# One gather in eighteen replaced by column copies on ScalarE and VectorE in a graph message-passing kernel

## The chip, the cores and the metric

The kernel runs on one core of one Trainium2 chip. The time is the device time of one execution in microseconds. The profile is of one execution on the same chip, with the same five engines that the text names throughout: PE (matmuls, with PEld for its weight loads), DVE (VectorE), ACT (ScalarE), POOL (GpSimd) and SP (which here only issues DMAs). Each engine takes its own instructions in order and waits for the others on semaphores.

## The reference

One layer of a graph network on 12,500 nodes with 64 features and 200,000 edges with 32 features, all float32. The edges are sorted by destination.

```python
msg_in = jnp.concatenate([nodes[row], nodes[col], edge_features], axis=-1)
messages = _mlp(msg_in, mW1, mb1, mW2, mb2)
aggregated = jax.ops.segment_sum(messages, col, num_segments=nodes.shape[0])
upd_in = jnp.concatenate([nodes, aggregated], axis=-1)
return _mlp(upd_in, uW1, ub1, uW2, ub2)
...
x = _layernorm(x + _L0_gnn_ref(x, src, dst, edge_attr_32, ...), axis=-1)
```

`_mlp(x, W1, b1, W2, b2)` is `relu(x @ W1 + b1) @ W2 + b2` with 128 hidden units. `row` is the source of an edge (random over all nodes), `col` its destination.

## The kernel before

The first message layer is split by its three inputs. A table A holds `x @ W1a` for every node (128 numbers each, in HBM), a table B holds `x @ W1b + b1`, and the edge features are multiplied by their part of W1 as they come. An edge's hidden vector is then relu(A[source] + B[destination] + edge part).

**Tiles.** 128 edges are one tile; 1,563 tiles. Six tiles (SUB) are one step, 261 steps; the text calls a step by its number s. Two steps (SUP, twelve tiles) share one selection and one load of edge features; they are number g, and j is 0 or 1 for the first or second step of the two.

**A step**, in the order in which the main loop (the `for s in range(last + 3)` loop) issues it:

- `gather` (L168), on POOL: one indirect DMA per tile takes 128 rows of A by the tile's source numbers. The first ten steps (XG) gather rows of x itself instead. 18 row buffers (ROWB) let POOL run ahead of the rest.
- `windows(s + 2)`, on SP: because destinations are sorted, a tile's destinations lie in a window of 32 rows of B. SP loads six window numbers into registers (L224) and issues six small DMAs into `rhs` (L229), each with a register operation that makes its address.
- `node_part(s)`: DVE adds the gathered rows to the matmul result, h = pc + xg (L276), ACT applies the relu (L277).
- `collect(s - 1)`, on PE: h times a selection matrix adds the tile's hidden vectors into a running sum by destination (L302), and a second matmul counts edges (L307). Six offsets come from registers that PE loads (L298).
- Every second step `select` makes a 0/1 matrix that tells the destination within the window (`l`, L196) and another for the sums (`sel`, L200), `load` brings edge features into the other rows of `l` (L215), and ACT makes a bfloat16 copy of `sel` (`counts`, L208). `loadd` (L184) brings the destination numbers that `select` compares.
- `edge_part(s + 1)`, on PE: one matmul per tile, `l` against `rhs` (L256), which gives B's row and the edge part together in `pc`. `pc` has two buffers.
- Updates: the running sums are closed 33 times, in steps that lie further apart at the start (47 steps) than at the end (4). An update takes two matmuls with 448 columns (`update`, L337 and L338), a relu, eight matmuls (`residual`, L346 and L347), DVE's statistics (L351, L353), a square root on ACT (L355), and the normalization (L364).

The order is written by hand (`manual_schedule`): each engine gets its instructions in the program's order, and only the semaphores are derived. During steps 11 to 50 PE also makes table B piece by piece (`chunk_b`).

Of the kernel before, what the change touches and what calls it, by code (L numbers as in the profile page):

```python
# [10 lines left out]
F32 = mybir.dt.float32  # L11
# [6 lines left out]
P = 128  # L18
# [6 lines left out]
SUB = 6  # L25
# [15 lines left out]
EARLY = NCH * P  # L41
GE = 26
BS = 11
UB = 4
NCOL = (-(-N // P) + UB) * P
UN = 448
# [17 lines left out]


@with_exitstack
def gnn_kernel(ctx: ExitStack, tc: tile.TileContext, x1T, x, eT, e_rows, src, dst, dst_row, wrow, wnext, whalf,
               mW1, mb1, mW2, mb2, uW1, ub1, uW2, ub2, out):

# [31 lines left out]
    K = len(UPD)  # L101

    src_s = const.tile([P, NT], I32, name="src_s")
    wint = const.tile([1, NTP], I32, name="wint")
    past = const.tile([1, 1], F32, name="past")

    xall = const.tile([P, -(-NB // NCH), HB * P], F32, name="xall")
# [30 lines left out]
    flag_i = const.tile([1, 1], I32, name="flag_i")  # L138
    usup = const.tile([1, K], I32, name="usup")
    ustep = const.tile([1, K], I32, name="ustep")  # L140
    woff = const.tile([1, NTP], I32, name="woff")
    wh = const.tile([P, NTP // 2], I32, name="wh")
    wa = const.tile([SUP, NSUP], I32, name="wa")
    wb = const.tile([SUP, NSUP], I32, name="wb")
# [9 lines left out]
    def tiles(s):  # L154
        return range(s * SUB, min((s + 1) * SUB, NT))

    def gather(s):

        if s >= XG or s % 2 == 0:
            buf = rows.tile([P, SUB, DH], F32, name="xg")  # L160
        else:
            buf = xg[s - 1][0]
        if s < XG:
            a = buf.rearrange("p k (b d) -> p (k b) d", d=D)[:, s % 2 * SUB:(s % 2 + 1) * SUB, :]
        else:
            a = buf.rearrange("p (b k) d -> p k b d", b=2)
        for i, t in enumerate(tiles(s)):
            nc.gpsimd.indirect_dma_start(  # L168
                out=a[:, i, :] if s < XG else a[:, i // 2, i % 2, :], out_offset=None, in_=A[:, :] if s >= XG else x[:, :],
                in_offset=bass.IndirectOffsetOnAxis(ap=src_s[:, t:t + 1], axis=0))  # L170
        xg[s] = buf, a

    with tc.tile_pool(name="sup", bufs=2) as sup, tc.tile_pool(name="work", bufs=2) as work, tc.manual_schedule():
        L, S, SB, xs, hs, pcs, sums = {}, {}, {}, {}, {}, {}, {}
        pt = psum.tile([P, SUB // 2, P], F32, name="pt", tag="sums")

# [63 lines left out]
        def parts(n):  # L240

            if n == SUB:
                return [(slice(0, 2), SUB // 2)]
            return [(slice(b, b + 1), (n - b + 1) // 2) for b in range(2) if n > b]

        def edge_part(s):

            n = len(tiles(s))
            g, j = divmod(s, SUP // SUB)

            pc = psum.tile([P, 2, 4, DH], F32, name="pc")[:, :, :SUB // 2]
            for i in range(n):
                k, b = divmod(i, 2)
                q, m = 64 * b, j * SUB // 2 + k

                nc.tensor.matmul(pc[:, b, k, :], L[g][q:q + 64, m, :], rhs[g % 2][q:q + 64, m, :],  # L256
                                 start=s >= XG or k == 0, stop=s >= XG)
            pcs[s] = pc

        def node_part(s):  # L260

            n = len(tiles(s))
            pc = pcs.pop(s)
            h = work.tile([P, 2, SUB // 2, DH], F32, name="h")
            if s < XG:
                xt = xs.pop(s)
                for i in range(n):
                    k, b = divmod(i, 2)
                    q = 64 * b
                    nc.tensor.matmul(pc[:, b, k, :], xt[q:q + 64, k, :], w1a[q:q + 64], start=False,  # L270
                                     stop=i + 2 >= n)
                nc.scalar.activation(h, pc, AF.Relu)
            else:
                a = xg.pop(s)[0].rearrange("p (b k) f -> p b k f", b=2)
                for b, m in parts(n):
                    nc.vector.tensor_tensor(h[:, b, :m], pc[:, b, :m], a[:, b, :m], op=ALU.add)  # L276
                    nc.scalar.activation(h[:, b, :m], h[:, b, :m], AF.Relu)  # L277
            hs[s] = h

        def opened(u):  # L280
# [37 lines left out]
        def close(u):  # L318

            ps, pn = sums.pop(u)  # L320
            nc.scalar.copy(sums_s[u % 2], ps)
            nc.scalar.copy(xw[u % 2][0:1, :UW], pn)

        us = {}

# [158 lines left out]
        for k, c in enumerate(range(0, NB, NCH)):  # L484
            chunk_a(c)
            if k == 0:
                chunk_b(0, [B0v, Bv])
            if k == 2:

                w0 = wint[:, :GE * SUP]  # L490
                nc.vector.tensor_scalar(past, w0[:, GE * SUP - 1:], float(EARLY - WIN), None, op0=ALU.is_gt)
                nc.vector.tensor_scalar(w0, w0, float(EARLY - WIN), None, op0=ALU.min)
                windows(0)
                windows(1)
            if k == 4:
                relative(0, 8 * SUP)
            if k == 6:
                offsets()
            if k == 9:
                select(0)  # L500
                load(0)
                counts(0)

        def rest(s):

            if s == 1:
                relative(8 * SUP, 8 * SUP + WCH)
            elif s == 2:
                relative(8 * SUP + WCH, NT)
                halves(4 * SUP, NTP // 2)  # L510
            elif s == BS:
                nc.sync.dma_start(wa, wrow.rearrange("o (p c) -> (o p) c", c=NSUP))
                nc.sync.dma_start(wb, wnext.rearrange("o (p c) -> (o p) c", c=NSUP))
                nc.scalar.dma_start(w2, mW2)
                nc.scalar.dma_start(u1a, uW1[D:2 * D, :])
                nc.scalar.dma_start(b2c, mb2.rearrange("(f o) -> f o", o=1))
                nc.vector.memset(uz[:D], 0.0)
                nc.vector.memset(ux[:D], 0.0)
                nc.vector.memset(eps, EPS)
                nc.vector.memset(ones, 1.0)  # L520
                nc.vector.tensor_copy(ux[D:], ident[D:, D:])
# [61 lines left out]
        for s in range(last + 3):  # L583
            g, j = divmod(s, SUP // SUB)
            while gathered < NSUB and frees(gathered) < s:
                gather(gathered)
                gathered += 1
            if s - 2 in due:
                norm(due[s - 2])
            if s + 2 < NSUB:  # L590
                windows(s + 2)
            if s < NSUB:
                node_part(s)
            if 1 <= s <= NSUB:
                collect(s - 1)
            if s + 1 in due:
                close(due[s + 1])
            if j == 0 and g + 1 < NSUP:
                select(g + 1)
                load(g + 1)  # L600
                counts(g + 1)
            if j == 1 and g + 2 < NSUP:
                loadd(g + 2)
            if chunks and s >= BS and chunks[0] < NCH + NB * (s + 1 - BS) / (SUP // SUB * (GE - 1) - BS):
                chunk_b(chunks.pop(0), [Bv])
            if s + 1 < NSUB:
                if s + 1 < XG:
                    transpose(s + 1)
                edge_part(s + 1)
            if s in due and due[s] + 1 < K:  # L610
                carry(due[s] + 1)
            if s in due:
                update(due[s])
            if s - 1 in due:
                residual(due[s - 1])
            if s + 2 in due:
                columns(due[s + 2])
            rest(s)
            if s - 2 in due:
                store(due[s - 2])  # L620
# [166 lines left out]
```

## Time and profile before

| | us |
|---|---|
| median of three runs | 1979.92 (1979.69 to 1980.9) |
| the profiled execution | 1980.06 |
| its span | 1978.3 |
| PE busy | 1520.7 (77%) |
| DVE busy | 554.1 (28%) |
| ACT busy | 359.1 (18%) |
| POOL busy | 1476.7 (75%) |
| granted TensorE clock, mean | 0.53 |
| DMA, mean | 105 GB/s |

Busy is the time in which the engine's datapath works on an instruction. Register operations, register loads and semaphore waits, which an engine's sequencer does itself, are not in it. The profile's groups give a line, an engine, an operation, the output and inputs, how often it ran, then busy time and mean duration in ns, and after the bar the idle time just before those instructions and what ended most of it.

### The profile page before, as it was taken

How to read it: one execution, taken by the hardware profiler on the slowest of the kernel's cores; microseconds unless marked ns; L12 is line 12 of the kernel's file. 1: busy time of each engine (PE TensorE's matmuls, PEld its weight loads, DVE VectorE, ACT ScalarE, POOL GpSimd, SP SyncE). 2: the span in 40 equal slices, each digit the busy share in tenths (PEclk: the TensorE clock that was granted, in tenths of full speed). 3: DMA queues.
4: the chain of work that ended last, by engine and by line, in shares of the span. 5: the costliest groups of instructions: out<-in, count | busy, mean ns of one | idle time of the engine just before them, and what ended most of it. 6: DMA issues, size and time to landing. Idle time of an engine off the chain costs nothing.

```text
span 1978.3 us, 34854 instructions
## 1 busy us (share of the span) xinstructions
PE 1520.7 (77%) x9218; PEld 1321.6 (67%) x9218; DVE 554.1 (28%) x1165; ACT 359.1 (18%) x550; POOL 1476.7 (75%) x1572
## 2 busy tenths in 40 slices
PE   3796898876757676776777777778778888888987
PEld 2696787765656665666666666667666777777766
DVE  1423333322222322222222232222222323323322
ACT  0221111211111111111111111111112112122121
POOL 7777777777777777777777777777777777777774
PEclk8655555555555555555555555555555555555555
DMA  8634454433333333333333333333333333333332
GB/s 207 181 97 120 130 134 126 115 103 92 98 94 95 94 98 98 94 96 99 96 98 96 101 92 100 101 97 99 100 99 98 99 103 97 101 102 100 101 103 63
DMA packets 244063, 208.45 MB, mean 105 GB/s; under 512 B 78233, under 2 KB 208370, under 8 KB 243875
## 3 DMA queue, kind: packets, MB, share of 16 engines
q0 software_dynamic: 50016, 100.57, 20.3%
q1 hardware_dynamic: 179312, 96.69, 17.8%
q10 hardware_dynamic: 14546, 8.93, 1.6%
q8 instruction: 88, 1.44, 0.3%
q14 instruction: 101, 0.82, 0.1%
HBM read 188.25 MB, written 17.69 MB: 104 GB/s over the span
## 4 chain that ended last, share of the span: by engine, by line
POOL 53%; issue 28%; PE 9%; DMA 7%; DVE 1%; SPq 1%; ACT 0%; ACTq 0%; DVEq 0%; POOLq 0%
POOL xg L168 53%; PE sums L302 4%; DMA xg<-tab_a,src_s 4%; PE pc L256 3%; DMA tab_a<-tb 1%; PE pb L410 1%; DMA l<-in_eT 1%; DMA w1b<-in_mW 1%; SPq L229 1%; PE pc L270 1%; PE pt L236 0%; PE cnt L307 0%; DMA rhs<-tab_b 0%; DMA xall<-in_x1T 0%; DVE tb L418 0%
## 5 line engine op out<-in xcount | busy, mean ns | idle before, releaser
L168 POOL DMA_INDIRECT xg<-tab_a,src_s x1503 | 1418.5, 944 | 460.5 <-issue 449.8
L302 PEld LDWEIGHTS sums<-sel,h 128*128 128x128 f32 x3126 | 669.6, 320 | 365.3 <-ACT h L277 316.4
L302 PE MATMUL sums<-sel,h 128*128 128x32 f32 x3126 | 689.5, 391 | 278.7 <-ACT h L277 265.9
L276 DVE TENSOR_TENSOR h<-pc,xg 128x768 f32<-128x768 f32 x252 | 239.5, 951 | 1043.7 <-DMA xg<-tab_a,src_s 812.8
L256 PE MATMUL pc<-rhs,l 64*128 64x128 f32 x3126 | 444.2, 439 | 95.4 <-DVE h L276 54.2
L256 PEld LDWEIGHTS pc<-rhs,l 64*128 64x128 f32 x3126 | 366.6, 318 | 120.2 <-DVE h L276 58.0
L277 ACT ACTIVATE h<-h 128x768 f32<-128x768 f32 x252 | 211.2, 839 | 1116.6 <-DVE h L276 1055.0
L196 DVE TENSOR_TENSOR l<-l,cps 128x768 f32<-128x768 int32 (+1 forms) x134 | 127.8, 954 | 98.5 <-DMA l<-in_dst_row 94.8
L208 ACT CAST selb<-sel 128x384 bf16<-128x384 f32 x131 | 66.7, 509 | 181.0 <-DVE sel L200 167.7
L346 PE MATMUL py<-ux,xw 128*128 128x64 f32 x264 | 84.5, 423 | 1.6 <-DVE h L276 1.6
L307 PE MATMUL cnt<-selb,one 128*1 128x32 bf16 x1563 | 85.3, 189 | 0.0
L347 PE MATMUL py<-u,hTu 128*128 128x64 f32 x264 | 82.9, 417 | 0.4 <-ACT hTu L339 0.4
L337 PE MATMUL pu<-sums_s,w2u 128*128 128x448 f32 x66 | 61.4, 1034 | 22.3 <-DVE h L276 21.6
L200 DVE TENSOR_TENSOR sel<-cps,drc 128x384 f32<-128x384 f32 x131 | 71.8, 548 | 20.0 <-PE sums L302 19.9
L346 PEld LDWEIGHTS py<-ux,xw 128*128 128x128 f32 x264 | 69.9, 324 | 9.5 <-issue 7.6
L347 PEld LDWEIGHTS py<-u,hTu 128*128 128x128 f32 x264 | 71.2, 329 | 0.6 <-ACT hTu L339 0.6
L168 POOL DMA_INDIRECT xg<-in_x,src_s x60 | 57.1, 952 | 19.1 <-issue 18.0
L307 PEld LDWEIGHTS <-one 128*1 128x1 bf16 x1563 | 54.3, 83 | 23.0 <-issue 8.7
L351 DVE BATCH_NORM_STATS2 st<-py 128x6 f32<-128x64 f32 x132 | 20.6, 218 | 160.6 <-PE py L347 157.0
L338 PE MATMUL pu<-xw,uz 128*128 128x448 f32 x66 | 55.2, 940 | 0.0
L410 PE MATMUL pb<-w1a,xall 64*128 64x128 f32 x196 | 23.5, 411 | 33.7 <-DVE tb L418 22.2
L410 PEld LDWEIGHTS pb<-w1a,xall 64*128 64x128 f32 x196 | 21.4, 306 | 35.4 <-DVE tb L418 23.5
(87 smaller groups left out, 437.6 us busy)
## 6 DMA issues: line engine op xcount, KB each, us to landing
l<-in_dst_row SPq DMA_DIRECT2D x262, 96.0 KB
l<-in_eT SPq DMA_DIRECT2D x262, 96.0 KB
rhs<-tab_b SPq DMA_DIRECT2D x1563, 16.0 KB
xg<-tab_a,src_s POOLq DMA_INDIRECT x1503
tab_b<-tb SPq DMA_DIRECT2D x13, 512.0 KB
tab_a<-tb ACTq DMA_DIRECT2D x12, 512.0 KB
out<-o SPq DMA_DIRECT2D x33, 128.0 KB
xw<-in_x1T SPq DMA_DIRECT2D x33, 113.8 KB
```

Of the source, the lines that this page charges most:

```text
L168: nc.gpsimd.indirect_dma_start(out=a[:, i, :] if s < XG else a[:, i // 2, i % 2, :], out_offset=None, in_=A[:, :] if s >= XG else x[:, :], ...
L196: nc.vector.tensor_tensor(l[r], l[r].bitcast(I32), node[r].unsqueeze(2).broadcast_to([r.stop - r.start, SUP // 2, P]), op=ALU.is_equal)
L200: nc.vector.tensor_tensor(s[:, :nt], slot.unsqueeze(1).broadcast_to([P, nt, WIN]), drc[:, g * SUP:g * SUP + nt].unsqueeze(2).broadcast_to( ...
L208: nc.scalar.copy(sb[:, :nt], S[g][:, :nt])
L256: nc.tensor.matmul(pc[:, b, k, :], L[g][q:q + 64, m, :], rhs[g % 2][q:q + 64, m, :], start=s >= XG or k == 0, stop=s >= XG)
L276: nc.vector.tensor_tensor(h[:, b, :m], pc[:, b, :m], a[:, b, :m], op=ALU.add)
L277: nc.scalar.activation(h[:, b, :m], h[:, b, :m], AF.Relu)
L302: nc.tensor.matmul(ps[:, bass.ds(ws[i], WIN)], h[:, i % 2, i // 2, :], S[g][:, k0 + i, :], start=False, stop=ends and i == n - 1)
L307: nc.tensor.matmul(pn[:, bass.ds(ws[i], WIN)], one, SB[g][:, k0 + i, :], start=False, stop=ends and i == n - 1)
L346: nc.tensor.matmul(py[:, i], xw[u % 2][:, i * P:(i + 1) * P], ux, start=True, stop=False)
L347: nc.tensor.matmul(py[:, i], hT[:, i * P:(i + 1) * P], u2, start=False, stop=True)
L410: nc.tensor.matmul(pb[:, h, i, :], xl[64 * h:64 * h + 64, i * P:(i + 1) * P], w[64 * h:64 * h + 64], start=True, stop=True)
```

## The change

One tile of every third step is no longer gathered. For s from 18 on with s % 3 == 2, the sixth tile of step s (`copied(s)`) gets its source features in another way. x transposed lies in SBUF as a table `xcol` with one column per node, on partitions 64 to 127. For each of the tile's 128 edges one column of 64 numbers is copied into `xo`, a 64 x 128 operand, and PE multiplies it with W1a in one more matmul into the same `pc`. The 128 copies are spread over three steps before they are used, some 43 at the end of each: 24 on ACT (CA), in two register loads of twelve source numbers and 24 copies, and 18 or 19 on DVE, as adds of a zero that lies in PSUM. The source numbers of these tiles are in `srow`, one row of 128 for each tile.

For a copied tile DVE's add leaves out the sixth tile, and ACT takes its relu straight from `pc`.

The selection, its edge load and its bfloat16 copy for group g + 2 are made in the second step of group g (before: for group g + 1, in the first step of g), and the destination load one step before that. The pool of selections has three buffers, where it had two. The first two groups are made ahead of the loop. The numbers `wint` and `woff` now lie in the unused partition 0 of `xcol`.

```diff
+CG = 3
+CF = 6 * CG
+CA = 24
+NCT = -(-(NSUB - CF) // CG)
...
+    xcol = const.tile([P, NB * P], F32, name="xcol")
+    wint, woff = (xcol[0:1, k * NTP:(k + 1) * NTP].bitcast(I32) for k in range(2))
+    srow = const.tile([NCT, P], I32, name="srow")
+    xo = [const.tile([P, P], F32, name=f"xo{k}") for k in range(2)]
...
+    def copied(s):
+        return s >= CF and s % CG == CG - 1 and len(tiles(s)) == SUB
...
-        for i, t in enumerate(tiles(s)):
+        for i, t in enumerate(tiles(s)[:SUB - copied(s)]):
...
+                c = copied(s) and i == n - 1
                 nc.tensor.matmul(pc[:, b, k, :], L[g][q:q + 64, m, :], rhs[g % 2][q:q + 64, m, :],
-                                 start=s >= XG or k == 0, stop=s >= XG)
+                                 start=s >= XG or k == 0, stop=s >= XG and not c)
+                if c:
+                    nc.tensor.matmul(pc[:, b, k, :], xo[s // CG % 2][q:q + 64], w1a[q:q + 64], start=False, stop=True)
...
+        def copies(s):
+            q, i = divmod(s + 2, CG)
+            t = q * CG + CG - 1
+            if t < CF or not t < NSUB or not copied(t):
+                return
+            k, e = i * P // CG, (i + 1) * P // CG
+            r = q - CF // CG
+            to = xo[q % 2]
+            def by_dve(o, i):
+                nc.vector.tensor_tensor(o, i, slot[D:, 0:1], op=ALU.add)
+            parts = []
+            for a, b, en, copy in ((k, k + CA // 2, ET.Activation, nc.scalar.copy),
+                                   (k + CA // 2, k + CA, ET.Activation, nc.scalar.copy),
+                                   (k + CA, e, ET.DVE, by_dve)):
+                _, v = nc.values_load_multi_w_load_instructions(
+                    srow[r:r + 1, a:b], engines=[en], min_val=0, max_val=N - 1,
+                    skip_runtime_bounds_check_because="sources are node numbers")
+                parts += [(copy, a + i, v[i]) for i in range(b - a)]
+            for copy, i, v in parts:
+                copy(to[D:, i:i + 1], xcol[D:, bass.ds(v, 1)])
...
+            if 3 <= s and (s - 3) * XCH < NB * P:
+                c = (s - 3) * XCH
+                e = min(c + XCH, NB * P)
+                nc.sync.dma_start(xcol[D:, c:e], x1T[1:, c:e])
...
-            if j == 0 and g + 1 < NSUP:
-                select(g + 1)
-                load(g + 1)
-                counts(g + 1)
-            if j == 1 and g + 2 < NSUP:
-                loadd(g + 2)
+            if j == 0 and g + 2 < NSUP:
+                loadd(g + 2)
+            if j == 1 and g + 2 < NSUP:
+                select(g + 2)
+                load(g + 2)
+                counts(g + 2)
...
+            copies(s)
             rest(s)
```

More of the change, by code (lines that the diff above doesn't have):

```diff
@@ L66, in gnn_kernel @@
 @with_exitstack
-def gnn_kernel(ctx: ExitStack, tc: tile.TileContext, x1T, x, eT, e_rows, src, dst, dst_row, wrow, wnext, whalf,
+def gnn_kernel(ctx: ExitStack, tc: tile.TileContext, x1T, x, eT, e_rows, src, src_row, dst, dst_row, wrow, wnext, whalf,
                mW1, mb1, mW2, mb2, uW1, ub1, uW2, ub2, out):
@@ L103, in gnn_kernel @@
     src_s = const.tile([P, NT], I32, name="src_s")
-    wint = const.tile([1, NTP], I32, name="wint")
+    xcol = const.tile([P, NB * P], F32, name="xcol")
+    wint, woff = (xcol[0:1, k * NTP:(k + 1) * NTP].bitcast(I32) for k in range(2))
+    srow = const.tile([NCT, P], I32, name="srow")
+    xo = [const.tile([P, P], F32, name=f"xo{k}") for k in range(2)]
     past = const.tile([1, 1], F32, name="past")
@@ L140, in gnn_kernel @@
     ustep = const.tile([1, K], I32, name="ustep")
-    woff = const.tile([1, NTP], I32, name="woff")
     wh = const.tile([P, NTP // 2], I32, name="wh")
@@ L171, in gather @@
         xg[s] = buf, a
-    with tc.tile_pool(name="sup", bufs=2) as sup, tc.tile_pool(name="work", bufs=2) as work, tc.manual_schedule():
+    with tc.tile_pool(name="sup", bufs=3) as sup, tc.tile_pool(name="work", bufs=2) as work, tc.manual_schedule():
         L, S, SB, xs, hs, pcs, sums = {}, {}, {}, {}, {}, {}, {}
@@ L274, in node_part @@
                 a = xg.pop(s)[0].rearrange("p (b k) f -> p b k f", b=2)
-                for b, m in parts(n):
-                    nc.vector.tensor_tensor(h[:, b, :m], pc[:, b, :m], a[:, b, :m], op=ALU.add)
-                    nc.scalar.activation(h[:, b, :m], h[:, b, :m], AF.Relu)
+                if copied(s):
+                    for b, m in ((0, SUB // 2), (1, SUB // 2 - 1)):
+                        nc.vector.tensor_tensor(h[:, b, :m], pc[:, b, :m], a[:, b, :m], op=ALU.add)
+                    hf = h.rearrange("p b k f -> p (b k) f")
+                    nc.scalar.activation(hf[:, SUB - 1], pc[:, 1, SUB // 2 - 1], AF.Relu)
+                    nc.scalar.activation(hf[:, :SUB - 1], hf[:, :SUB - 1], AF.Relu)
+                else:
+                    for b, m in parts(n):
+                        nc.vector.tensor_tensor(h[:, b, :m], pc[:, b, :m], a[:, b, :m], op=ALU.add)
+                        nc.scalar.activation(h[:, b, :m], h[:, b, :m], AF.Relu)
             hs[s] = h
@@ L499, in gnn_kernel @@
             if k == 9:
-                select(0)
-                load(0)
-                counts(0)
+                for g in range(2):
+                    select(g)
+                    load(g)
+                    counts(g)
+        XCH = 2048
         def rest(s):
+            if 3 <= s and (s - 3) * XCH < NB * P:
+                c = (s - 3) * XCH
+                e = min(c + XCH, NB * P)
+                nc.sync.dma_start(xcol[D:, c:e], x1T[1:, c:e])
             if s == 1:
@@ L508, in rest @@
             elif s == 2:
+                nc.sync.dma_start(srow, src_row[CF * SUB + SUB * CG - 1::SUB * CG, :][:NCT])
                 relative(8 * SUP + WCH, NT)
@@ L769 @@
         "src": sp.reshape(-1, P).T[:, :NT],
+        "src_row": sp.reshape(-1, P),
         "dst": dp[:EPAD].reshape(-1, P).T[:, :NT],
```

## The prediction

> **What bounds the kernel now.** I read the chain of waits first, then the costliest groups, then single rows of the trace around one step.
>
> ```profile
> POOL 53%; issue 28%; PE 9%; DMA 7%; DVE 1%; SPq 1%; ACT 0%; ACTq 0%; DVEq 0%; POOLq 0%
> ...
> L168 POOL DMA_INDIRECT xg<-tab_a,src_s x1503 | 1418.5, 944 | 460.5 <-issue 449.8
> ...
> L276 DVE TENSOR_TENSOR h<-pc,xg 128x768 f32<-128x768 f32 x252 | 239.5, 951 | 1043.7 <-DMA xg<-tab_a,src_s 812.8
> ...
> L277 ACT ACTIVATE h<-h 128x768 f32<-128x768 f32 x252 | 211.2, 839 | 1116.6 <-DVE h L276 1055.0
> ```
>
> POOL and its "issue" are 81% of the chain. A gather is 944 ns with 306 ns of issue behind it, (1418.5 + 460.5) / 1503 = 1.250 us, with no other wait. DVE's add waits 812.8 us for gathers, ACT waits for that add. So POOL sets the pace: six gathers, 7.50 us a step. DVE (28%) and ACT (18%) look idle. But register work is not counted as busy, and the change is made of register work.
>
> **What goes.** Tiles 20, 23, ... 257 are copied: 80 gathers, 1503 to 1423. 80 x 1.250 = **100.0 us** off POOL, which needs 17 gathers in three steps: 21.25 us, 7.08 a step.
>
> **What comes.** In each of 240 steps (16 to 255) a third of 128 columns: on ACT 24 copies of 64x1 and two register loads of 12 words, on DVE 18 or 19 adds and one load of as many words. Before each copy stands one register operation that makes its address. ACT's rows of the program grow by about 50 a step, DVE's by 39. None of this exists on these engines before, so I take SP's and PE's rows, which do the same for the windows. These are answers by line, durations min/median/max in ns:
>
> ```profile
> L328 SPq TENSOR_LOAD <-usup x33: 268/279/288, 371.0 to 1950.5; - x33
> ...
> L224 SPq TENSOR_LOAD <-wint x1: 1272/1272/1272, 1006.8 to 1006.8; - x1
> ...
> L224 SPq TENSOR_LOAD <-wint x1: 720/720/720, 1012.4 to 1012.4; - x1
> ...
> L298 PEldq TENSOR_LOAD <-woff x261: 774/1463/2073, 79.3 to 1959.6; - x131
> ...
> L302 PEldq FUSED_REGOPS  x6: 37/37/37, 1005.8 to 1006.5; - x6
> ```
>
> A load of one word takes 0.28 us. One of six takes 0.72 in even steps and 1.27 in odd ones, and PE's alternate in the same way (0.82, 1.47). The words of even steps begin at a multiple of 16 bytes (48 a pair of steps), those of odd steps 8 bytes beside one. 0.28 + 5 x 0.20 = 1.28: off the boundary it seems to go word by word, on it in pieces. The new words begin at columns 0, 42 and 85 of a row: the first third on a boundary, the others not. So two loads in three steps take about 0.75 (estimate, by the 0.72 row), four take 0.28 + 11 x 0.20 = 2.5: 1.5 + 10.0 = **11.5 us per three steps** on ACT. Bounds: if only the first six words go singly, 1.27 + 0.4 = 1.7, sum 8.3; if loads on several engines slow each other, as PE's maximum of 2.07 against 1.47 hints, 11.5 x 1.4 = 16.
>
> [...]
>
> A copy with its register operation: PE's six register operations start within 0.7 us, with a matmul issued after each, 0.7 / 5 = 0.14. The datapath would be quicker, by ACT's two copies back to back:
>
> ```profile
> 1057.72 0.54 ACT L321 COPY sums_s<-sums 128x480 f32<-128x480 f32 x1
> 1058.16 0.54 ACT L322 COPY xw<-cnt 1x480 f32<-1x480 f32 x1
> ```
>
> 0.54 us each, 0.44 apart: about 0.10 overlaps. Less 480 elements at 0.83 ns (the slope between ACT's 128x256 and 128x768 rows, 417 and 842 ns), a copy is 0.14, every 0.05. So issue decides: 72 x 0.14 = **10.1 us**. [...]
>
> The rest of ACT's issue (relus, selection casts, update instructions and their waits, some 8 in three steps at 0.11): 0.9. **ACT: 11.5 + 10.1 + 0.9 = 22.5 us in three steps, 7.5 a step**, against POOL's 7.08. DVE: loads 1.4 + 2 x 4.2 (0.28 + 18 x 0.20, and a tenth more, since a one-word load takes 546 ns on DVE and 475 on ACT at the end of the trace), 56 adds at 0.16 (nearest row: its four small aggregates in 0.36 us, 0.07 apart, plus a register operation with its gap, 0.09), other issue 2.2 with four semaphore waits before each add: 9.8 + 9.0 + 2.2 = 21.0, 7.0 a step. ACT becomes the bound: the register loads lie on the same in-order sequencer as the copies and the next relu, and behind that relu waits PE's L302, and behind it everything on PE.
>
> **From step to end.** DVE's adds for steps 16 and 256, and for an update's second step:
>
> ```profile
> 180.12 0.96 DVE L276 TENSOR_TENSOR h<-pc,xg 128x768 f32<-128x768 f32 x1 [1.91 <-DMA xg<-tab_a,src_s]
> ...
> 1895.06 0.96 DVE L276 TENSOR_TENSOR h<-pc,xg 128x768 f32<-128x768 f32 x1 [3.90 <-DMA xg<-tab_a,src_s]
> 1903.93 0.94 DVE L276 TENSOR_TENSOR h<-pc,xg 128x768 f32<-128x768 f32 x1
> ...
> 1933.88 0.95 DVE L276 TENSOR_TENSOR h<-pc,xg 128x768 f32<-128x768 f32 x1
> ```
>
> Before, 240 steps took 1753.8, 7.31 each: about 40 us behind the gathers at step 20, the adds ran at 6.2 a step until 375 and caught up. At 7.5 they never do. 180.1 + 240 x 7.5 = 1980.1, plus the tail after step 256 (1978.3 - 1933.9 = 44.4) is 2024.5.
>
> Updates: in 33 steps DVE's statistics wait 5.42 us for PE (L351) and ACT's square root for them (adds 8.87 apart, above). ACT's loads can run under that wait, its 24 copies (3.4) cannot, and the next step's loads win some back: about 2.5 net, 33 x 2.5 = 82. Ends: 0 if all is covered; 8.5 (loads also exposed, since four statistics and four aggregates stand queued before them), 280. Sum 2106.
>
> **Edits that cost nothing.** PE gets 80 matmuls more (12 halves of L256 in 1.66 us, two each: 80 x 0.28 = 22 us), beside ACT; PE is busy 77%; without that cover 22. PE's last edge matmul of a copied step now waits for ACT's copies, with the sums of the next step queued behind it; some 2 us of PE idling in one step of three, hidden while PE has 1.7 a step to spare. Splitting relu and add in copied steps: 0.2 us of datapath per three steps. The column table is 3.2 MB in seven transfers on SP's queue in steps 3 to 9, past the window loads there; SP gives each about 0.4 us (L215: two in 0.79) and the dropped gathers save 5.2 MB: 0, at most 5. Selections and loads one step sooner: the destination load stays one step before the selection, the edge load gains a step, which ends PE's 28.6 us of waiting for it (L256), none of it on POOL's chain: 0 to -3. The two first selections move ahead of the loop: 2.7 us of DVE that was due anyway.
>
> The profiled run was 1980.06 for a span of 1978.3, 1.8 around it; the median of three is 1979.92. Forecast: 2106 + 1.8, about **2108**.
>
> **Rivals.**
> - POOL stays the bound (0.23). [...] Then 1978.3 - 100.0, some 15 of lag where updates come every four steps, +1.8: **1895**. It decides from 6.97 a step down: (1978.3 - 44.4 - 82 - 180.1) / 240. Against it: the 1.27 us rows.
> [...]
> - DVE's wait in updates is not covered (0.12): 2024.5 + 280 + 1.8 = **2306**. For it: the eight queued instructions; against it: DVE's semaphore waits for the next add already run while L364 is in work.
> - The lines cancel, no change (0.03): ACT at 7.0.
>
> My forecast has 0.48. **Range 1915 to 2350**: it leaves out about half of the first rival and over half of the second, 0.12 and 0.08. A difference under 0.2% (4 us) could not be told from none. Faster 0.23, same 0.03, slower 0.74.
>
> **What would show it.** ACT's register loads at 2.5 us in two steps of three and 0.75 in the third; register operations 0.14 apart; adds 7.5 apart, no longer waiting for DMA but for PE or nothing; POOL idle on ACT's or DVE's progress once the 18 row buffers are full. If POOL's gathers still follow each other at 1.25 to the end and adds wait for them, I am wrong; the loads' durations will say by which term.

## The result, and the profile after

The changed kernel takes **2248.24 us** (median of 4 runs, 2244.23 to 2251.4) where the kernel before takes 1980.41 beside it: 1.135 times as long, 95% interval 1.134 to 1.136. The forecast was 2108; direction and range held, but the loss is 268 us where 128 were forecast. The profiled execution's span is 2249.6.

The profile's page of the changed kernel, the chain of waits (by engine, then by line) and the groups that answer to the three shown of before, with the new ones:

```profile
issue 25%; PE 20%; ACTq 16%; ACT 11%; POOL 10%; DVE 9%; DMA 5%; DVEq 2%; SPq 1%; POOLq 0%
ACTq L362 16%; POOL xg L180 10%; ACT xo L367 8%; PE sums L324 5%; PE pc L269 4%; DVE xo L356 3%; PE pu L382 2%; PE py L391 2%; PE pu L383 2%; DMA xg<-tab_a,src_s 2%; PE py L392 2%; DVEq L362 2%; DVE l L208 1%; DVE h L298 1%; DMA tab_a<-tb 1%
...
L180 POOL DMA_INDIRECT xg<-tab_a,src_s x1423 | 1342.8, 944 | 665.6 <-issue 412.6
L367 ACT COPY xo<-xcol 64x1 f32 x5760 | 608.8, 188 | 829.0 <-issue 827.5
L356 DVE TENSOR_TENSOR xo<-xcol,cps 64x1 f32<-64x1 f32 x4480 | 587.5, 159 | 648.7 <-issue 647.2
...
L298 DVE TENSOR_TENSOR h<-pc,xg 128x768 f32<-128x768 f32 (+1 forms) x172 | 163.2, 949 | 51.6 <-issue 18.4
...
L299 ACT ACTIVATE h<-h 128x768 f32<-128x768 f32 (+1 forms) x172 | 143.7, 836 | 58.5 <-DVE h L298 36.2
...
L396 DVE BATCH_NORM_STATS2 st<-py 128x6 f32<-128x64 f32 x132 | 20.6, 219 | 262.7 <-PE py L392 262.7
```

POOL has fallen from 53% of the chain to 10%, and ACTq, ACT's sequencer, stands where it was nearly nothing: 16%, all of it line 362, the register loads. The add (now L298, and L292 in copied steps) waits for hardly anything: 15 us in all for gathers, where it waited 812.8. What a gather costs has not changed (944 ns; 80 are gone), but POOL's idle time has grown by 205 us, and the view of waits for POOL says why:

```profile
POOL xg L180 <- issue: 430.6, 1391, 6.6
POOL xg L180 <- DVE cps L206: 123.8, 17, 13.4
POOL xg L180 <- DVE h L298: 92.9, 24, 11.9
```

(us in all, times, longest.) In these 41 waits POOL stands until DVE has done an add, or the instruction behind it (L206), and so freed row buffers: the 18 of them are full. POOL is the one that waits now.

**The new operations.** The register loads by their source line (minimum, median, maximum ns; first and last start):

```profile
L362 ACTq TENSOR_LOAD <-srow x480: 780/2630/3996, 181.9 to 2207.1; - x160
L362 DVEq TENSOR_LOAD <-srow x240: 1570/4298/5636, 180.9 to 2201.4; - x120
```

And the pace of DVE in three regular steps (start, duration, then in brackets the idle time before it):

```profile
607.68 0.96 DVE L298 TENSOR_TENSOR h<-pc,xg 128x768 f32<-128x768 f32 x1 [0.17 <-DMA xg<-tab_a,src_s]
609.50 2.36 DVE L356 TENSOR_TENSOR xo<-xcol,cps 64x1 f32<-64x1 f32 x18 [0.87 <-issue]
611.90 0.89 DVE L292 TENSOR_TENSOR h<-pc,xg 128x384 f32<-128x384 f32 x2
...
617.56 2.35 DVE L356 TENSOR_TENSOR xo<-xcol,cps 64x1 f32<-64x1 f32 x18 [3.18 <-issue]
...
620.63 0.96 DVE L298 TENSOR_TENSOR h<-pc,xg 128x768 f32<-128x768 f32 x1 [0.24 <-DMA xg<-tab_a,src_s]
625.25 2.48 DVE L356 TENSOR_TENSOR xo<-xcol,cps 64x1 f32<-64x1 f32 x19 [3.66 <-issue]
627.98 0.96 DVE L298 TENSOR_TENSOR h<-pc,xg 128x768 f32<-128x768 f32 x1 [0.24 <-DMA xg<-tab_a,src_s]
```

The adds start 4.2, 8.7 and 7.3 us apart. Between the add at 620.63 and the 19 copies behind it DVE's datapath is idle 3.66 us, "issue", and this is its register load:

```profile
L362 DVEq TENSOR_LOAD <-srow x1: 4405/4405/4405, 620.7 to 620.7; - x1
```

It began with the add and took 4.4 us. DVE goes from copies to add to load to copies, with nothing else in the way. Whether DVE or ACT sets the pace of regular steps is tested below.

**Where the 268 us are.** I take the starts of the adds of steps 16, 51 and 256: 180.9, 461.0 and 2209.7. In steps 16 to 50, with one update in them, PE also makes table B: 280.1 us, where the kernel before took 216.9. From 51 to 256 there are 205 steps and 30 updates in 1748.7 us. A step far from updates takes **7.00 us** (mean of 36 steps between 52 and 114: from the fourth step behind an update on, in whole groups of six). The rest, 1748.7 - 205 x 7.00 = 314, is **10.5 for each update** (the expectations below say 10.2). The kernel before, split in the same way, has 7.50 and 0.0: POOL's six gathers set its pace, and the row buffers hide the updates. So of the 275 us lost between steps 16 and 256, 63 lie ahead of step 51; behind it regular steps won 102 us and updates lost 314. Against the forecast (7.5 a step and 2.5 an update) regular steps are 102 us shorter, updates 234 longer and the steps up to 50 some 15 longer. With 180.9 ahead and 39.9 behind, this is the span.

One such update, from the timeline:

```profile
698.64 0.63 ACT L384 ACTIVATE hTu<-pu,ub_s 128x448 f32<-128x448 f32 x1 [4.06 <-PE pu L383]
...
707.08 0.63 DVE L396 BATCH_NORM_STATS2 st<-py 128x6 f32<-128x64 f32 x4 [8.95 <-PE py L392]
...
708.02 0.30 ACT L400 ACTIVATE sd<-mv,eps 128x4 f32<-128x4 f32 x1 [3.54 <-DVE mv L398]
...
712.33 2.48 DVE L356 TENSOR_TENSOR xo<-xcol,cps 64x1 f32<-64x1 f32 x19 [4.35 <-issue]
713.69 2.51 ACT L367 COPY xo<-xcol 64x1 f32 x24 [5.38 <-issue]
...
715.06 1.10 DVE L409 TENSOR_SCALAR o<-py,mv,rs 128x64 f32<-128x64 f32 x4
716.08 0.95 DVE L298 TENSOR_TENSOR h<-pc,xg 128x768 f32<-128x768 f32 x1
716.21 1.36 PEld L269 LDWEIGHTS pc<-rhs,l 64*128 64x128 f32 x12 [6.54 <-DVE o L409]
```

And the loads of the same step, by source line between 706 and 710 us:

```profile
L362 DVEq TENSOR_LOAD <-srow x1: 4397/4397/4397, 707.8 to 707.8; - x1
L362 ACTq TENSOR_LOAD <-srow x1: 2715/2715/2715, 708.0 to 708.0; - x1
```

DVE has nothing to do for 8.95 us while it waits for the statistics' input, yet its load starts at 707.8, when the instructions in front of it have gone. ACT's starts at 708.0, with the square root that had waited 3.54. So 4.4 us of load and 2.5 of copies follow the wait one after the other, the normalization stands behind them, and PE, whose next matmul needs the buffer that the normalization reads, waits 6.54 us more. The matching add starts 20.4 us after the last one. In the mean of the 32 such intervals it was 8.9 before the change; now it is 17.9.

### The profile page after: what moved, and what is told of

The parts are those of the page before. It is cut to its first block, busy times and chain, and to the rows that moved or that the text cites. A ratio compares the mean times of both kernels' runs of the same rounds, so it can differ in the third digit from the quotient of the medians.

```text
span 2249.6 us, 55923 instructions
## 1 busy us (share of the span) xinstructions
PE 1529.6 (68%) x9378; PEld 1319.5 (59%) x9378; DVE 1137.5 (51%) x5725; ACT 970.2 (43%) x6390; POOL 1400.9 (62%) x1492
## 4 chain that ended last, share of the span: by engine, by line
issue 25%; PE 20%; ACTq 16%; ACT 11%; POOL 10%; DVE 9%; DMA 5%; DVEq 2%; SPq 1%; POOLq 0%
ACTq L362 16%; POOL xg L180 10%; ACT xo L367 8%; PE sums L324 5%; PE pc L269 4%; DVE xo L356 3%; PE pu L382 2%; PE py L391 2%; PE pu L383 2%; DMA xg<-tab_a,src_s 2%; PE py L392 2%; DVEq L362 2%; DVE l L208 1%; DVE h L298 1%; DMA tab_a<-tb 1%
## 5 line engine op out<-in xcount | busy, mean ns | idle before, releaser
L180 POOL DMA_INDIRECT xg<-tab_a,src_s x1423 | 1342.8, 944 | 665.6 <-issue 412.6
L367 ACT COPY xo<-xcol 64x1 f32 x5760 | 608.8, 188 | 829.0 <-issue 827.5
L356 DVE TENSOR_TENSOR xo<-xcol,cps 64x1 f32<-64x1 f32 x4480 | 587.5, 159 | 648.7 <-issue 647.2
L269 PE MATMUL pc<-rhs,l 64*128 64x128 f32 x3126 | 419.0, 432 | 178.4 <-DVE o L409 134.4
L269 PEld LDWEIGHTS pc<-rhs,l 64*128 64x128 f32 x3126 | 345.0, 312 | 200.9 <-DVE o L409 138.4
L272 PE MATMUL pc<-w1a,xo 64*128 64x128 f32 x160 | 62.5, 492 | 205.4 <-ACT xo L367 196.2
L298 DVE TENSOR_TENSOR h<-pc,xg 128x768 f32<-128x768 f32 (+1 forms) x172 | 163.2, 949 | 51.6 <-issue 18.4
L272 PEld LDWEIGHTS pc<-w1a,xo 64*128 64x128 f32 x160 | 40.0, 309 | 227.2 <-ACT xo L367 217.0
L299 ACT ACTIVATE h<-h 128x768 f32<-128x768 f32 (+1 forms) x172 | 143.7, 836 | 58.5 <-DVE h L298 36.2
L292 DVE TENSOR_TENSOR h<-pc,xg 128x384 f32<-128x384 f32 (+1 forms) x160 | 71.1, 486 | 7.1 <-PE pc L272 2.8
```

The lines of the kernel that those rows point to most:

```text
L180: nc.gpsimd.indirect_dma_start(out=a[:, i, :] if s < XG else a[:, i // 2, i % 2, :], out_offset=None, in_=A[:, :] if s >= XG else x[:, :], ...
L356: nc.vector.tensor_tensor(o, i, slot[D:, 0:1], op=ALU.add)
L367: copy(to[D:, i:i + 1], xcol[D:, bass.ds(v, 1)])
```

## The experiments

Two theories for the updates: the loads are **shut out** by the instruction in front that waits, and so lie bare behind it; or the excess is **PE's own chain** in the update, which only comes to light in a slower kernel. For the regular steps: the loads' price is set by where the source numbers lie, or the copies themselves are too dear. "Regular step" and "per update" below are worked out from the adds as above, in each run's trace. For a count that begins one step sooner or later behind an update they move by at most 0.1 and 0.9 us.

| kernel | us | ratio to before, 95% | regular step | per update |
|---|---|---|---|---|
| before | 1980.4 | 1 | 7.50 | 0.0 |
| changed | 2248.2 | 1.134 to 1.136 | 7.00 | 10.5 |
| all copies ahead of the update | 2066.8 | 1.042 to 1.046 | 7.00 | 4.7 |
| loads alone ahead | 2105.6 | 1.060 to 1.064 | 7.00 | 5.9 |
| ahead of its second part alone | 2214.5 | 1.116 to 1.120 | 7.01 | 9.4 |
| aligned loads | 1887.0 | 0.952 to 0.955 | 6.96 | 0.7 |
| aligned and ahead | 1883.9 | 0.950 to 0.953 | 7.06 | 0.0 |
| no copies at all | 1885.0 | 0.950 to 0.954 | 7.05 | 0.2 |
| aligned, DVE's off again | 2145.5 | 1.081 to 1.084 | 6.93 | 7.8 |
| aligned, ACT's off again | 2219.3 | 1.118 to 1.122 | 7.19 | 8.5 |
| copies a step sooner | 2242.3 | 1.131 to 1.135 | 7.00 | 10.4 |
| every second step copied | 1981.9 | 0.999 to 1.001 | 6.58 | 4.7 |
| before, selections sooner | 1983.7 | 1.001 to 1.002 | 7.50 | 0.0 |

### Copies ahead of the update

```diff
             if s in due and due[s] + 1 < K:
                 carry(due[s] + 1)
+            copies(s)
             if s in due:
                 update(due[s])
...
-            copies(s)
             rest(s)
```

> The changed kernel, with the copies of a step (register loads and all) issued ahead of that step's update instead of at the step's end. Theory 'loads shut out': an update costs 10.2 us, not 2.5, because the register loads on ACT and DVE do not start until the update's own waits (for hTu, for the statistics) are over, so that loads and copies lie one after the other behind these waits. Then with the loads ahead of the waits the excess of an update falls from 10.2 to 3 to 5 us, and the time by some 32 x 6 = 190 us, to about 2060; the interval of the step after an update falls from 17.9 to 11 to 13. Rival 'PE's chain': the excess is the update's chain through PE (sums, pu, py) which only lies later in a slower kernel: then 2240 to 2260, no change. Regular steps stay at 7.1 by both.

2066.77. The same loads and copies, the same regular step; only their place against the update's waits differs, and an update costs 4.7 us in place of 10.5, 181 us in all. DVE's wait for the statistics' input, in the changed kernel and here:

```profile
DVE st L396 <- PE py L392: 262.7, 33, 11.3
DVE st L396 <- PE py L392: 70.9, 22, 9.9
```

The work that had stood behind the wait now fills it. The rival is out. What makes up the 4.7 us that are left, no run shows.

### Loads on a 16-byte boundary

The thirds of a tile's 128 source numbers (4 bytes each) began at words 0, 42 and 85. Now they begin at 0, 44 and 88 (so DVE's shares become 20, 20 and 16).

```diff
-            k, e = i * P // CG, (i + 1) * P // CG
+            k, e = 44 * i, min(44 * (i + 1), P)
```

> The changed kernel, with the row of source numbers cut at 0, 44 and 88 instead of 0, 42 and 85, so that each register load starts on a 16-byte boundary (20, 20 and 16 columns on DVE for 18, 19 and 19). If the boundary alone sets a load's price, ACT's loads take 0.8 us in all steps (2.6 in two of three now) and DVE's about 1.6 (4.3 now in two of three), regular steps fall from 7.09 to about 6.6 to 7.0 with POOL's gathers the bound, and an update costs 10.2 - 4 = about 6: 1.8 + 180 + 240 x 6.9 + 32 x 6 + 40 = about 2070 with 1.25 us gathers and less lag, down to 1930. Rival 'the copies themselves are the price': then regular steps stay above 7.0, updates at 9 to 10, and the time at 2180 or more.

**1886.96**, 361 us less than the changed kernel and 93 less than before the change, by one line. The loads by source line:

```profile
L362 ACTq TENSOR_LOAD <-srow x480: 769/794/1463, 179.2 to 1840.8; - x160
L362 DVEq TENSOR_LOAD <-srow x240: 1096/1355/2450, 178.2 to 1839.6; - x120
```

These medians mix loads of several lengths on DVE. By length, twelve words take 0.79 us on ACT and twenty 1.38 on DVE, against 2.65 for twelve and 4.40 for nineteen off the boundary. I expected 2070 down to 1930 and had left a rest of 6 us on each update; the time is below that. POOL's seventeen gathers in three steps (7.08 a step) are the bound again. The interval that held 17.9 us is still 13.1 us in the mean, but behind it a step can take less than 7.08 (4.2 for the next one), so that almost nothing of an update is left (0.7 us): the row buffers carry POOL over it. Steps 16 to 50 take 216.9 us, as before the change. POOL's waits in this run:

```profile
POOL xg L180 <- issue: 429.5, 1395, 4.5
POOL xg L180 <- DMA xg<-tab_a,src_s: 14.6, 48, 0.3
POOL xg L180 <- DVE xo L356: 5.8, 19, 0.3
```

The 217 us of waiting for DVE are gone; what is left is 0.3 us at a time.

### Both, and no copies at all

Aligned loads and copies ahead of the update; and, for the floor, the changed kernel without loads, copies and their matmul:

```diff
-                c = copied(s) and i == n - 1
+                c = False
...
-            copies(s)
```

> Both edits together: aligned loads, and the copies issued ahead of the update. Theory 'loads shut out and unaligned' explains all of the loss: then POOL is the bound again but for the ends of updates, and the time is 1890 to 1940, less than before the change (1980). If something else (the wait of PE's last edge matmul for the copies, the split relu) carries part of the loss, it stays above 1980.

> The changed kernel without the register loads, the copies and the matmul with xo: the last tile of every third step has neither gather nor copy, so its source features are left out of the sum. This is the most that the dropped gathers can bring. By the gathers' row (80 at 1.25 us) it is 1980 - 100 = 1880; if POOL is not what the dropped time was waiting for, it stays nearer 1980. Against the changed kernel's 2248 it also says what loads, copies and the extra matmul cost in all: about 370 us.

1883.94 (1890 to 1940 expected) and 1884.98. The floor is the before time less 94.5 us (100.0 by the gathers' row), and the full computation with aligned loads stands on it: 5,760 copies on ACT and 4,480 on DVE with their loads cost nothing once POOL sets the pace. Moving them ahead as well is worth 3 us, about what can't be told from none. These two aligned kernels beat both kernels of this case.

### One engine's loads off the boundary again

In the aligned kernel, in two steps of three, one engine's load begins one word earlier and leaves the first word unused:

```diff
+                w = int(i > 0 and en == ET.DVE)
                 _, v = nc.values_load_multi_w_load_instructions(
-                    srow[r:r + 1, a:b], engines=[en], min_val=0, max_val=N - 1,
+                    srow[r:r + 1, a - w:b], engines=[en], min_val=0, max_val=N - 1,
...
-                parts += [(copy, a + i, v[i]) for i in range(b - a)]
+                parts += [(copy, a + i, v[w + i]) for i in range(b - a)]
```

For ACT, `en == ET.Activation`.

> The kernel with aligned loads, but DVE's load starts one word earlier in two steps of three (21 or 17 words off the boundary, the first unused), so that only DVE's loads are slow again (4.9 and 4.0 us; ACT's stay at 0.8). Theory 'DVE sets the pace of the changed kernel' (three steps: loads 10.3, 56 adds at 0.13 = 7.3, waits and selections 3.6: 21.2, 7.1 a step): regular steps return to about 7.0, the updates keep most of their 10 us since the load lies behind the statistics' wait, and the time is 2110 to 2200. Rival 'ACT sets it', as the forecast had it: then the time stays under 1950.

> The kernel with aligned loads, but ACT's two loads start one word earlier in two steps of three (13 words off the boundary, 2.86 us each; DVE's stay aligned). ACT's issue is then (4 x 2.86 + 1.6 + 7.3 + 0.9) / 3 = 7.1 a step. By the theory that DVE set the pace and ACT stood close behind it, this costs less than DVE's loads, mainly in regular steps: 2000 to 2090. Rival 'ACT carries the loss': nearly all of it returns, 2150 to 2250, and the run with DVE's slow loads is fast.

DVE's alone: 2145.54, regular steps 6.93: as expected. ACT's alone: 2219.28, and that I had not expected (2000 to 2090). Its regular step (7.19) is near the 7.1 that I had worked out for loads of thirteen words (2.86 us); with twelve (2.65) it would be some 4 x 0.21 / 3 = 0.28 shorter, 6.9 (an estimate). So in the changed kernel DVE and ACT need nearly the same for a regular step, and neither can be called the one that sets its 7.00. What I had wrong is the update: ACT's loads alone make it cost 8.5 us, DVE's 7.8. The thirteenth word adds to ACT's loss, by some 205 x 0.28 = 57 us at most (an estimate). The losses, 258 and 332 us over the aligned kernel, don't add up to the 361 of both: the two engines' loads lie beside each other. PE's view of waits, DVE's loads slow:

```profile
PE sums L324 <- ACT h L299: 174.1, 96, 5.0
PE pc L269 <- DVE o L410: 173.6, 31, 7.5
```

and ACT's slow:

```profile
PE pc L272 <- ACT xo L368: 268.0, 78, 6.6
PE sums L324 <- ACT h L299: 265.0, 120, 6.2
PE pc L269 <- DVE o L410: 70.1, 21, 3.9
```

In the first PE waits for the normalization `o` (31 times, once an update); in the second for the copies and the relu.

### Loads alone, and one part of the update alone

The loads ahead of the update with the copies left at the step's end (`copies` returns its copying as a function `go`); and loads and copies ahead of the second part alone:

```diff
+            go = copies(s)
             if s in due:
                 update(due[s])
...
-            copies(s)
+            if go:
+                go()
```

```diff
             if s - 1 in due:
+                copies(s)
                 residual(due[s - 1])
...
-            copies(s)
+            if s - 1 not in due:
+                copies(s)
```

> The changed kernel with only the register loads of a step issued ahead of its update; the copies stay at the step's end, behind the update's waits. The loads are the same, unaligned. By the theory 'the loads are shut out by the wait', an update keeps the 2.5 us of copies over the 4.7 of the run with everything ahead, near 7 us, and the time is 2067 + 32 x 2.4 = 2145, between 2100 and 2160. If it is the copies that the wait shuts out, nothing is gained: 2220 to 2250.

> The changed kernel with loads and copies ahead of the update's second part alone (the eight matmuls and DVE's statistics), not ahead of its first part (the relu on ACT). In the second part both engines' loads stand behind a wait, in the first only ACT's. So most of the 181 us that the move ahead of both parts gained should come: 60 to 90%, 2085 to 2140. If ACT's wait for the first matmuls is the price, little comes: 2180 to 2240.

Loads alone: 2105.56, 143 of the 181 us. The wait shuts out loads above all; the copies are the smaller part (1.2 us an update for 2.4 expected).

Ahead of the second part alone: 2214.54, only 34 us, a miss; it lies where the rival had it, that ACT's wait in the first part is the price. DVE's view of waits, in the changed kernel and here:

```profile
DVE rs L406 <- ACT sd L400: 0.7, 2, 0.4
DVE rs L406 <- ACT sd L400: 139.6, 33, 11.3
```

DVE now waits for ACT's square root. On ACT the loads now stand in front of the square root, and when ACT comes from the first part with slow loads and copies of its own, that is late. Where the loads of both steps are slow (12 of 32 updates), the interval grew from 17.6 to 20.4 us; in the other 20 it fell by 3.2. Both parts of the update stand in ACT's one line of instructions.

The mirror, ahead of the first part alone, was run four times, and each time on chips on which the kernel before took 2755 to 2809 us (last section). It stood there between 3023 and 3085, 1.095 to 1.099 times before, beside 3042.87 for the changed kernel in the series that had both. This says nothing about chips where before takes 1980, so how the 181 us split between the two parts stays open.

> The mirror of the run that moved loads and copies ahead of the update's second part and gained 34 us, not 110 or more: here they are moved ahead of the first part alone, whose relu on ACT waits for PE. Theory now: ACT's queue is one line; what stands behind the first wait (8 us of loads and copies) delays the next relu and the square root behind it, and there is no room for a second such pack between the two waits. Then taking the first pack out of the line brings more than the second did: 70 to 130 us, 2120 to 2180. If both waits were worth about the same, or the gain needs both at once: 30 us or less, 2210 to 2240.

> The same kernel as in the run before (loads and copies ahead of the update's first part alone), on a chip where the kernel before takes its usual 1980 us; in that run the kernel before took 2758, and small instructions stood 0.7 and 1.4 us apart at places, so it says nothing of the two waits. Expected as there: with one line on ACT, 2120 to 2180; if both waits are worth the same or the gain needs both at once, 2210 to 2240.

> Loads and copies ahead of the update's first part alone, now beside the changed kernel itself and the aligned one on one chip, so that the three can be compared there even if the kernel before should take 2755 us again. With one line on ACT, it takes 70 to 130 us less than the changed kernel; if only both moves together gain, 30 us less or nothing.

> Loads and copies ahead of the update's first part alone, once more, for a chip on which the kernel before takes 1980. With one line on ACT: 2120 to 2180. If only both moves together gain: 2210 to 2240. If the kernel before takes 2755 again, 2990 to 3050, and the question stays open.

### Copies a step sooner, selections alone, every second step

```diff
-            q, i = divmod(s + 2, CG)
+            q, i = divmod(s + 3, CG)
```

> The changed kernel with the copies for a tile made one step sooner (in steps t - 5 to t - 3 for t - 4 to t - 2), loads as they are. PE's wait for xo before its last edge matmul (205 us in 80 steps, 2.5 each) then ends before PE comes to it. If that wait is hidden, as the forecast had it, because DVE and ACT set the pace anyway: 2225 to 2255. If it is on the path: up to 200 less.

2242.33, 6 us less. PE's wait for `xo` in the changed kernel

```profile
PE pc L272 <- ACT xo L367: 196.2, 71, 4.6
```

is gone from PE's waits here, so it was hidden, as the forecast had it.

The kernel before with the selections, their loads and casts one step sooner, and nothing else:

```diff
-            if j == 0 and g + 1 < NSUP:
-                select(g + 1)
...
-            if j == 1 and g + 2 < NSUP:
+            if j == 0 and g + 2 < NSUP:
                 loadd(g + 2)
+            if j == 1 and g + 2 < NSUP:
+                select(g + 2)
...
```

> The kernel before with only the other part of the change: selections, edge loads and their casts one step sooner, three selection buffers. No gather is dropped. POOL's gathers are the bound, so no change to be seen: 1976 to 1981. If the wait of PE for the edge load had delayed the end, up to 28 us less.

1983.71 against 1980.39 (1976 to 1981 expected): 3 us more, a small loss (1.001 to 1.002) and no gain.

Aligned and ahead, with every second step's last tile copied (`CG = 2`, `CA = 36`, halves at 0 and 64):

> Aligned loads and early copies, and every second step's last tile copied (64 columns a step: 36 on ACT in loads of 20 and 16, 28 on DVE), which drops 124 gathers. POOL alone: 1884 - 44 x 1.25 = 1829. DVE a step: load 7 x 0.27 = 1.9, adds 28 x 0.13 = 3.6, waits and selections 1.2: 6.7. ACT: 2.4 + 36 x 0.101 = 3.6, rest 0.5: 6.5, and an update's waits come on top. If the engines' sums are right, ACT and DVE have no room left for the updates, and the time is 1860 to 1930: hardly better than copying every third. If POOL stays the bound, 1830 to 1845.

1981.91, above the 1860 to 1930 expected. The regular step came near what I had worked out (6.58 for 6.7). POOL's eleven gathers in two steps need 6.88, so DVE and ACT can catch up by only 0.3 us a step, and each update adds 4.7 us, some 140 in all. One tile in three steps is the better size: aligned and ahead, an update there adds nothing.

## Why the prediction was right and wrong

- **POOL as the bound before, 100.0 us in the dropped gathers**: right; without any copies 94.5 are gained.
- **The loads' durations**: right for the layout as it was. ACT 2.65 and 0.80 us (2.5 and 0.75 forecast), DVE 4.4 and 1.6 (4.2 and 1.4). A word cost 2.65 / 12 = 0.22 us off the boundary and, in the aligned kernel, 0.79 / 12 = 0.066 on it. I used that difference as a cost and didn't ask what the kernel would be without it: 361 us less, more than the whole loss of 268.
- **Copies 0.14 apart on ACT, 0.16 on DVE**: 24 take 2.51 us on ACT, 0.10 apart, and 19 take 2.48 on DVE, 0.13 apart, register operations between them. ACT's copies are 72 x 0.101 = 7.3 us for 10.1. (The 0.14 was the mean of five distances in PE's row, four of 0.115 us and one of 0.21; the shorter one came nearer.) One copy lasts 188 ns in the profile, but two of them start 101 apart. The second rival of the range (chance 0.14) had copies that cost more than the forecast's 10.1 us; no run shows such a price, they took 7.3. (DVE's wait, at 2306, is the third.)
- **ACT becomes the bound at 7.5**: too long by 0.7. ACT's sum with the measured terms is (4 x 2.65 + 2 x 0.80 + 7.3 + 0.9) / 3 = 6.8; the 0.9 in it is still the forecast's estimate, which no run shows alone. What had made it 7.5 are the copies, 10.1 us where they took 7.3. For loads of thirteen words the sum gives 7.1, and 7.19 was seen with DVE's loads fast. DVE's 7.0 was right (6.93 with ACT's loads fast). Both together take 7.00, a little less than POOL's 7.08, so regular steps are not where the change loses. The direction "DVE and ACT become the bound, POOL waits for row buffers" was right.
- **Updates at 2.5 us**: this is the step that failed. "ACT's loads can run under that wait, its 24 copies (3.4) cannot." The loads can't either: in the traces above and below a load starts only once the waiting instruction ahead of it has started (ACT's at 708.0 with a square root at 708.02, PE's at 1004.9 with a weight load at 1004.87), and an update cost 10.5 us. Putting the loads alone ahead of the waits brought 143 us back. The mechanism stood in the text as the bound 8.5 ("loads also exposed, since four statistics and four aggregates stand queued before them") and as the rival at 2306 with a chance of 0.12. I weighed it low because DVE's semaphore waits for the next add overlap with running work: in the trace of before three of them start at 1902.9 to 1903.1, while the normalization (L364) runs 1.10 us from 1902.91. But those overlap with an instruction that has started; a load behind an instruction that waits is another case. The trace of before did hold that case. PE's register load in an update began only with the weight load that had waited 1.48 us in front of it:

```profile
1004.87 0.50 PEld L337 LDWEIGHTS pu<-sums_s,w2u 128*128 128x128 f32 x2 [1.48 <-DVE h L276]
L298 PEldq TENSOR_LOAD <-woff x1: 822/822/822, 1004.9 to 1004.9; - x1
```

- **PE's wait for `xo`, the selections, the column table at nothing**: the first two were run and are hidden (6 us, and 3 the other way). The table was not tried alone; step 16 starts 0.8 us later than before, so there is little in it.
- **The first rival's 6.97**: this is the step at which the time would be what it was before, and not the one from which POOL decides; the 1895 named there needs (1895 - 1.8 - 44.4 - 82 - 180.1) / 240 = 6.61.
- **Signs**: loads as forecast; register operations 0.10 apart, not 0.14; adds at 7.00, not 7.5, and no longer waiting for gathers; POOL idle until DVE moves on, as forecast.

The two errors partly cancel (-102 for regular steps and +234 for updates), so that the total lies nearer than its parts by luck.

## What to carry to other kernels

Before a row of numbers is read into registers, place each read on a 16-byte boundary: here that one line was worth 361 us, and it turned a loss of 13% into a gain of 5% on the chips where the kernel before takes 1980 (on the others see below). A register load ran here in the program's order, behind whatever its engine waited for. Put it ahead of an instruction that waits (143 us here), and ahead of all the waits of a stage: ahead of the second alone it brought 34 us for loads and copies together. Count it as bare time where it stands behind. When a sum is made of stages, check the rare stage as hard as the common one: 30 updates lost 314 us here, while the 205 steps around them got faster.

## What the runs showed of the hardware

**Loads by length and start.** These are medians by length, from the changed kernel, the aligned one and the one with every second step copied. On the boundary ACT's loads of 12, 16 and 20 words take 0.79, 1.04 and 1.29 us, and DVE's of 16, 20 and 28 words 1.12, 1.38 and 1.90, some 0.26 for each four words. DVE's eighteen words on the boundary, in the changed kernel, take 1.61, longer than twenty: this fits sixteen words at 1.12 and two singly at 0.22 to 0.23, 1.57 (an estimate). Off it, 12 take 2.65 and 19 take 4.40, 0.22 to 0.23 for each word, with starts on an 8-byte boundary (ACT from word 42, DVE from 66: 2.65 and 4.40) or on a 4-byte one (from 85 and 109: 2.64 and 4.39) alike.

**On some chips the order turns round.** In four series, on three chips, the kernel before took 2755 to 2809 us; on the chips of the other runs it took 1980. There the aligned kernel is *slower* than before, 2979.53 us, 1.078 times (1.074 to 1.081; 0.95 to 1.05 expected), and the changed one 3042.87, 1.102 times:

> The changed kernel itself, as the measure for its two neighbours in this series: 2248 on a chip where the kernel before takes 1980; where that takes 2755, the ratio of 1.135 need not hold, since small instructions stand apart there and this kernel has 10,000 more of them: 1.10 to 1.20.

> The kernel with aligned loads again: 1887 on a chip where the kernel before takes 1980. If before takes 2755, the copies' small instructions may no longer hide: between 0.95 and 1.05 of it.

The copies of ACT by source line (register operation, then copy), the aligned kernel on the usual chip:

```profile
L367 ACTq FUSED_REGOPS  x5760: 46/46/52, 181.1 to 1844.0; - x199
L367 ACT COPY xo<-xcol x5760: 182/188/190, 181.2 to 1844.1; 64x1 f32 x199
```

and on such a chip, with a stretch of its timeline:

```profile
L367 ACTq FUSED_REGOPS  x5760: 3/46/1404, 363.2 to 2940.3; - x199
L367 ACT COPY xo<-xcol x5760: 182/188/190, 363.4 to 2940.4; 64x1 f32 x199
```

```profile
566.36 0.19 ACT L367 COPY xo<-xcol 64x1 f32 x1 [1.13 <-issue]
567.07 0.19 ACT L367 COPY xo<-xcol 64x1 f32 x1 [0.52 <-issue]
568.48 0.19 ACT L367 COPY xo<-xcol 64x1 f32 x1 [1.22 <-issue]
```

No copy is slower there (188 ns), and no gather (944); but register operations and copies stand 0.5 to 1.4 us apart in groups of about ten, and these groups begin most often 90 to 120 of ACT's instructions apart. Over 0.4 us pass from the start of one of these instructions to that of the next 1,172 times on ACT, 827 us in all; in the aligned kernel on the usual chip this never happens. ACT's idle time just before its copies that is put down to issue is 879.7 us there and 276.8 on the usual chip. That a kernel with some 21,500 more instructions (55,929 for 34,356 without copies) pays for it more often is my estimate from these counts. What holds the instructions up there, no run shows. There is no trace of the kernel before on such a chip: its further run fell on a usual one, and took 1980.07 beside 1980.85.

> The kernel before, for a trace of it on a chip where it takes 2755 us: it should show the same gaps of 0.65 to 0.75 us between small instructions, in groups about every 100 instructions of an engine, and POOL waiting for row buffers (DVE's progress) though the gathers still follow each other at 1.25 us elsewhere. On a chip where it takes 1980 it shows no such gaps.


